# Small operations moved between engines, and the edges of two scan layers, in a four-layer state-space kernel

## The chip, the cores and the metric

The kernel runs on one core of a Trainium2 chip. A core has five engines that run beside each other, each through its own instructions in order: TensorE (PE, with its weight loads as PEld), VectorE (DVE), ScalarE (ACT), GpSimd (POOL) and SyncE (SP), which here issues all DMAs. The metric is the device time of one execution in microseconds, as the median of several runs.

## The reference

The input is 8 images of 48 x 48 pixels with 96 channels, in float32. Four layers follow each other, each as `x = x + layer(group_norm(x))`.

Layers 0 and 3 (`ss2d` in the kernel) are 2D selective scans. A projection gives 2 x 192 channels, u and z. u goes through a 3 x 3 depthwise convolution and a SiLU. The image is then read as a sequence in four directions (rows, columns, and both backward), and in each of them a recurrence with 16 states a channel is run:

```
dA = exp(dl[..., None] * A)
h = h * dA + (dl * u)[..., None] * Bv[:, :, None, :]
y = einsum('bkdn,bkn->bkd', h, Cv)
...
y = sum of the four directions, back in image order, plus D * u
y = (y - mean(y)) * rsqrt(var(y) + 1e-5) * norm_w + norm_b
out = (y * silu(z)) @ out_proj.T
```

`dl` (softplus of a small projection), `Bv` and `Cv` are projections of u. Layer 2 (`lines`) does the same recurrence along each row or column separately, restarts it at every line, gates each direction by silu(z), projects it and adds it to x. Layer 1 (`spectral`) upsamples by Fourier, applies a small network and downsamples.

## The kernel before

The four layers run one after the other. An image (a "job") has 4 directions of 5 blocks each: `BLKS` cuts it into four blocks of 10 rows or columns (480 pixels) and one of 8 (384). A scan layer is thus a list of 8 x 4 x 5 blocks, made in `scans`, direction after direction.

A block has 192 channels x 16 states = 3072 sequences, kept as 24 units of 128 partitions. It goes through 8 slots of 3 units (two slots are a turn `t`, 4 turns are a block, 160 slots an image). For each turn the code issues, in this order by engine:

- VectorE: three recurrences of two units (`scan`, L263, `tensor_tensor_scan` in place in the tile dbu), and between them the products dl * u * B (`make_dbu`, L235).
- ScalarE: the decays exp(dl * A) into a PSUM tile (`make_da`, L255), two units at a time, with two buffers, so that the decays of a scan can be made while the scan before it runs; and a copy of B into PSUM (`copy_b`, L216).
- GpSimd: a part of the products dl * u * B (L235, the table `ON_POOL`), and h * C in place (`make_hc`, L276).
- TensorE: the sum over the 16 states, as matmuls with a 0/1 matrix into the PSUM tile y (`reduce`, L296 and L298). It comes one turn after the scans.
- SyncE: loads of B and C for the next block (`load_bc`, L204) and of dl and dl * u (`load_dd`, L192), broadcast over partitions.

Everything else is fitted in by `aside`, which is called once a slot. It issues the loads of that slot, takes one step of the generator `beside` (which `side(job)` makes), then runs the steps of `stage1` that prepare the block after next (`plan`), then the steps that `done` has put aside. Nothing is scheduled by the machine: the order in which the code issues instructions is the order of each engine, and the framework only adds the waits that the data and the buffers need. PSUM tiles of the name "side" have one buffer.

In `ss2d`, `side(job)` does for the image before: `post`, the norm over channels, gate and output projection; and for the image after: load, `front` (group norm) and `conv` (the 3 x 3 convolution as nine 128-column matmuls a half block, L481, with SiLUs at L490 and L492). `post` has two loops over the 5 blocks. The first takes the mean (L504), subtracts it (L507), squares (L510), sums by matmul (L515) and copies the variance (L518), five steps a block; then square root and reciprocal of the whole image (L520, L522). The second, from slot 30 on, again takes five steps a block:

```
step 1: z <- zd, xi <- x by DMA (L528, L530); PE repeats 1/sigma over the partitions (L534)
step 2: DVE y *= norm_w * 1/sigma, two instructions (L538)
step 3: POOL y *= z (L541); PE norm_b part of the projection (L544)
step 4: PE projection of y (L547)
step 5: DVE xi += result (L550)
then:   store of xi by DMA (L552), before step 1 of the next block
```

The tile zin has one buffer, xi has two. The last image has no image after it, so its `post` runs after the scans, alone. The first image's `front` and `conv` run before the scans, alone.

In `lines`, `done` multiplies y by silu(z) on VectorE (L785), `project` multiplies by the output weights a slot later (L794), and `add` adds the result to x on VectorE, one more slot later (L800 for direction 0, with the bias; L802 for the others). Directions 2 and 3 go by columns, so x is then read and written with a stride.

Of the kernel before, what the change touches and what calls it, by code (L numbers as in the profile page):

```python
# [17 lines left out]
DH = 96  # L18
# [57 lines left out]
def vss_stack_kernel(ctx: ExitStack, tc: tile.TileContext, i: dict, out: bass.AP):  # L76
# [89 lines left out]
    def scans(dirs, restart, a, pools, ps, stage1, opening, done, side, tail):  # L166
# [9 lines left out]
                  for job in range(nb) for k in range(NK)  # L176
# [171 lines left out]
        for t, (b, q) in enumerate(turns):  # L348
            at, nblk = 2 * t, t // (NG // 2)
            if q == 0:  # L350
                if nblk + 2 < len(blocks):
                    plan(blocks[nblk + 2], at)
                if b.k == 0 and b.first:
                    beside = side(b.job)
# [24 lines left out]
            if q == NG // 2 - 1 and b.k == NK - 1 and b.last:  # L379
                for _ in beside:  # L380
                    while tail:
                        tail.pop(0)()
# [47 lines left out]
    def ss2d(l, xin, xout, b0=0):  # L430
# [65 lines left out]
        def post(b):  # L496
            y = yss[b]
            var = small.tile([CH, L // CH], F32, tag="var", name="var")
            for r0, nr in BLKS:
# [20 lines left out]
            nc.scalar.activation(var, var, AF.Sqrt, bias=eps5[:CH])  # L520
            yield
            nc.vector.reciprocal(var, var)  # L522
            yield
            for r0, nr in BLKS:
# [7 lines left out]
                for c in range(n // CH):  # L532
                    at = r0 * W // CH + c
                    nc.tensor.matmul(pr[:DH, c * CH:(c + 1) * CH], lhsT=var[:, at:at + 1].to_broadcast([CH, DH]),  # L534
                                     rhs=wc["ident"], start=True, stop=True)
                yield
# [4 lines left out]
                nc.gpsimd.tensor_mul(y[:, :, s], y[:, :, s], z[:, :, :n])  # L541
# [8 lines left out]
                nc.vector.tensor_add(xi[:, :n], xi[:, :n], po[:C, :n])  # L550
                yield
                nc.sync.dma_start(xout[b][:, s], xi[:, :n])  # L552

        def side(job):
            used = 0
            more = job + 1 < nb
            if more:
# [9 lines left out]
            if more:  # L567
# [6 lines left out]
                yield from conv(job + 1)  # L574
# [74 lines left out]
    def lines(xin, xout):  # L649
# [131 lines left out]
        def done(b, half, y):  # L781
# [7 lines left out]

            def project():  # L790
                got["o"] = ps("s1", 2)
                t = gated.pop(b)
                for h in range(2):
                    nc.tensor.matmul(got["o"][:C, :n], lhsT=wo[:, b.k, h, :], rhs=t[:, h, :n], start=(h == 0), stop=(h == 1))  # L794
# [27 lines left out]
        scans(dirs, True, a, pools, ps, stage1, opening, done, side, tail)  # L822
# [289 lines left out]
```

## Time and profile before

| what | value |
|---|---|
| median of 3 runs | 19549.3 us (19545.86 to 19551.5) |
| the profiled execution | 19542.61 us, span 19540.6 us |
| first scan layer: first scan, last scan's end | 148.7 us, 5902.6 us |
| `lines`: first scan of the layer | 7397.6 us |
| last scan layer: first scan | 13675.7 us |
| VectorE L263, the recurrences | 5760 instructions, 11858.2 us busy |
| GpSimd L276, h * C | 3840 instructions, 11439.8 us busy |
| ScalarE L255, the decays | 11520 instructions, 7414.7 us busy |
| TensorE L296 and L298 | 30720 records, 4983.6 and 4942.9 us busy |

The page gives the busy time of each engine, the groups of instructions by source line with the idle time before them and what ended it, and the chain of work that ended last. The windows view sums busy time in stretches of time, the waits view lists who waited for whom, and the timeline lists instructions in order; its columns are start, duration, engine, line, operation, output and inputs, and the idle time before it with its releaser in brackets. A float32 matmul shows as two records. Most of the time lies in three long, even scan stages (two of `ss2d`, one of `lines`), so what one image costs there counts eight times.

### The profile page before, as it was taken

The numbers are of one execution on the slowest core, as the hardware profiler recorded it, in microseconds if no ns is written. First come the engines' busy times: TensorE is split into PE (matmuls) and PEld (weight loads), VectorE is DVE, ScalarE is ACT, GpSimd is POOL, SyncE is SP. The second block draws the span as 40 slices with busy tenths as digits, with TensorE's granted clock in tenths as the row PEclk, the third lists the DMA queues.
The fourth block names the chain that finished last, engine by engine and source line by source line (L and its number), as shares of the span: only waits on it lengthen the run. The fifth ranks groups of instructions, "written<-read, shape, count | busy, mean of one in ns | idle before, by whom it ended". The sixth has DMA issues, their size and how long they took to land. (4 is left out here: it accounts for less than half of the span.)

```text
span 19540.6 us, 172984 instructions
## 1 busy us (share of the span) xinstructions
PE 15237.1 (78%) x53500; PEld 4370.8 (22%) x53500; DVE 16831.8 (86%) x11281; ACT 14144.5 (72%) x22222; POOL 16028.7 (82%) x9825
## 2 busy tenths in 40 slices
PE   6777777777767887888888988887677777777776
PEld 1211211211214552222222222222121121121121
DVE  6999999999992228999999999996999999999997
ACT  5877777877772227788788777885778778778775
POOL 6999999999991007888888888886999999999997
PEclk6777776776767777888878888887677677667765
DMA  3444444444443324434434444443444444444443
GB/s 130 160 162 158 162 160 163 158 163 158 156 170 48 50 45 145 145 141 150 150 139 147 147 146 145 144 149 112 158 163 160 159 164 157 160 162 161 156 165 123
DMA packets 768486, 2829.44 MB, mean 145 GB/s; under 512 B 235724, under 2 KB 298668, under 8 KB 640926
## 3 DMA queue, kind: packets, MB, share of 16 engines
q1 hardware_dynamic: 767558, 2818.38, 43.1%
q8 instruction: 422, 6.91, 0.1%
q14 instruction: 506, 4.15, 0.1%
HBM read 2371.42 MB, written 446.69 MB: 144 GB/s over the span
## 5 line engine op out<-in xcount | busy, mean ns | idle before, releaser
L263 DVE TENSOR_TENSOR_SCAN dbu<-ps_da,dbu 128x962 f32<-128x962 f32 (+3 forms) x5760 | 11858.2, 2071 | 897.9 <-ACT ps_da L255 895.7
L276 POOL TENSOR_TENSOR dbu<-dbu,bc 128x1440 f32<-128x1440 f32 (+1 forms) x3840 | 11439.8, 2985 | 1040.6 <-DVE dbu L263 814.0
L255 ACT ACTIVATE ps_da<-dd,w_l_a 128x481 f32<-128x481 f32 (+3 forms) x11520 | 7414.7, 648 | 2729.7 <-DVE dbu L263 2523.7
L296 PE MATMUL ps_y<-dbu,w_red 128*32 128x480 f32 (+1 forms) x23040 | 4983.6, 752 | 3051.0 <-POOL dbu L276 3047.3
L298 PE MATMUL ps_y<-dbu,w_red 128*32 128x480 f32 (+1 forms) x7680 | 4942.9, 752 | 0.0
L235 DVE TENSOR_TENSOR dbu<-dd,ps_b 128x1440 f32<-128x1440 f32 (+5 forms) x3840 | 4645.3, 1210 | 320.1 <-ACT ps_b L216 275.7
L235 POOL TENSOR_TENSOR dbu<-dd,bc 128x480 f32<-128x480 f32 (+3 forms) x1920 | 3026.2, 1576 | 61.9 <-DMA bc<-bcd 36.6
L296 PEld LDWEIGHTS ps_y<-dbu,w_red 128*32 128x32 f32 x23040 | 742.7, 125 | 7009.7 <-POOL dbu L276 5283.6
L216 ACT COPY ps_b<-bc 128x480 f32<-128x480 f32 (+1 forms) x3360 | 1798.4, 535 | 300.7 <-DVE dbu L235 271.3
L722 PE MATMUL ps_s<-xpad,w_l_cw 128*128 128x480 f32 (+1 forms) x2560 | 1747.2, 834 | 2.3 <-ACT xpad L124 1.6
L481 PE MATMUL ps_side<-xpad,w_l_cw 128*128 128x480 f32 (+1 forms) x2880 | 1617.4, 690 | 4.6 <-ACT xpad L124 4.5
L255 ACT ACT_TABLE_LOAD x970 | 1244.5, 1283 | 17.1
L113 POOL MEMSET w_l_cw<- 128x1760 f32 (+1 forms) x3 | 5.8, 1942 | 1326.7 <-DVE x L932 1321.3
L422 POOL TENSOR_TENSOR dds<-dds,u 96x480 f32<-96x480 f32 (+1 forms) x640 | 793.6, 1240 | 259.9 <-ACT dds L611 259.9
L593 PE MATMUL ps_s<-u,w_l_xp 96*38 96x480 f32 (+1 forms) x1280 | 957.2, 888 | 4.1 <-ACT dds L587 3.0
L583 PE MATMUL ps_s<-bcl,dtw 6*96 6x480 f32 (+1 forms) x1280 | 878.4, 775 | 86.3 <-ACT dds L587 82.2
L270 POOL COPY carry<-dbu 128x3 f32<-128x3 f32 x2048 | 386.4, 189 | 582.6 <-DVE dbu L263 570.2
L292 PE MATMUL ps_y<-ysum,w_ident 96*96 96x480 f32 (+1 forms) x960 | 740.7, 861 | 113.7 <-ACT ysum L634 112.8
L481 PEld LDWEIGHTS ps_side<-xpad,w_l_cw 128*128 128x128 f32 x2880 | 571.0, 222 | 1115.0 <-issue 916.4
L722 PEld LDWEIGHTS ps_s<-xpad,w_l_cw 128*128 128x128 f32 x2560 | 525.8, 210 | 1087.1 <-issue 938.1
L298 PEld LDWEIGHTS ps_y<-dbu,w_red 128*32 128x32 f32 x7680 | 683.1, 125 | 0.0
L763 PE MATMUL ps_s<-xpad,w_l_inz 96*96 96x480 f32 (+1 forms) x640 | 505.7, 924 | 86.9 <-ACT dds L757 69.2
(146 smaller groups left out, 12586.2 us busy)
## 6 DMA issues: line engine op xcount, KB each, us to landing
dd<-dd SPq DMA_DIRECT2D x512, 1443.0 KB
bc<-bcd SPq DMA_DIRECT2D x1536, 480.0 KB
dd<-dd SPq DMA_DIRECT2D x256, 1440.0 KB
dd<-dds SPq DMA_DIRECT2D x512, 360.8 KB
dd<-dd SPq DMA_DIRECT2D x128, 1155.0 KB
bc<-bcd SPq DMA_DIRECT2D x384, 384.0 KB
dd<-dds SPq DMA_DIRECT2D x256, 360.0 KB
dd<-dd SPq DMA_DIRECT2D x64, 1152.0 KB
```

What stands on the lines that cost most here:

```text
L216: nc.scalar.copy(bps[t][:, :b.n], bcs[t][:, 0, :b.n])
L235: engine.tensor_mul(o, du, by.unsqueeze(1).to_broadcast([P, hi - lo, b.n]))
L255: nc.scalar.activation(da[:, at:at + b.m], b.got[half][:, u % 3, 0, :], AF.Exp, scale=a[:, b.k, ci:ci + 1])
L263: nc.vector.tensor_tensor_scan(db, da, db, 0.0, ALU.mult, ALU.add)
L276: nc.gpsimd.tensor_mul(h, h, bcs.pop(2 * t + sub)[:, 1, :n].unsqueeze(1).to_broadcast([P, 3, n]))
L296: nc.tensor.matmul(y[32 * g:32 * g + 32, :n], lhsT=wc["red"][:, :32], rhs=hc[:, g, b.at], start=False, stop=(slot == 3))
L298: nc.tensor.matmul(y[DH:, :n], lhsT=wc["red"][:, 32:], rhs=hc[:, 2, b.at], start=(slot == 0), stop=(slot == 3))
L422: nc.gpsimd.tensor_mul(rows(du, n), rows(dt, n), u)
L481: nc.tensor.matmul(pu[:, :n], lhsT=flat[:, at:at + P], rhs=xpad[:, r0 + dy:r0 + dy + nr, dx:dx + W], start=(tap == 0), stop=(tap == 8))
L583: nc.tensor.matmul(got["p"][:DH, :n], lhsT=dtw[2 * NS:, b.k, half, :], rhs=b.bcl[2 * NS:, :n], start=True, stop=True)
L593: nc.tensor.matmul(got["p"][:NBC, :n], lhsT=w[f"{l}_xp"][:, b.k, half, :], rhs=u[:, half], start=(half == 0), stop=(half == 1))
L722: nc.tensor.matmul(got["u", half][:, :n], lhsT=flat[:, at:at + P], rhs=shifted(off), start=(tap == 0), stop=(tap == 3))
```

## The change

In `ss2d`:

- The norm weight is multiplied into the rows of the output weights once a layer, on ScalarE. In `post`'s second loop y * z on GpSimd now stands in step 1, and 1/sigma is applied after the projection: step 2 copies 1/sigma from PSUM (ACT), step 3 projects y * z (PE), step 4 multiplies the two (DVE), step 5 sums xi, the norm_b part and the result in PSUM by four matmuls, two of them with the identity (PE); a copy on ACT takes it out, followed at once by the store of xi and by step 1 of the next block.
- `post` takes a list of blocks. The last image's blocks 4 to 1 go through it one by one beside the last direction, two steps a slot; block 0 alone runs after the scans. For that the order of directions is 0, 1, 3, 2, so that the last one goes by rows, backward, and finishes block 4 first.
- `conv` of the first image does three blocks before the scans; the last two, two fifths, stand beside the first two blocks of scans, two steps a slot.

In `lines`, x joins the projection in PSUM as an identity matmul, and ScalarE copies the sum into x (with the bias for direction 0), in place of VectorE's addition.

```diff
--- before.py
+++ after.py
@@ -163,7 +163,7 @@
         yield
 
 
-    def scans(dirs, restart, a, pools, ps, stage1, opening, done, side, tail):
+    def scans(dirs, order, restart, a, pools, ps, stage1, opening, done, side, tail):
 
 
 
@@ -173,7 +173,7 @@
 
 
         blocks = [Block(job, k, blk, n == 0, n == len(BLKS) - 1, dirs[k][1])
-                  for job in range(nb) for k in range(NK)
+                  for job in range(nb) for k in order
                   for n, blk in enumerate(range(len(BLKS))[::-1 if dirs[k][1] else 1])]
         for b in blocks:
             b.columns(restart)
@@ -350,7 +350,7 @@
             if q == 0:
                 if nblk + 2 < len(blocks):
                     plan(blocks[nblk + 2], at)
-                if b.k == 0 and b.first:
+                if b.k == order[0] and b.first:
                     beside = side(b.job)
             scan(t, 0)
             if t > 0:
@@ -376,7 +376,7 @@
             copy_b(at + 4)
             finish(at + 1)
             aside(at + 1)
-            if q == NG // 2 - 1 and b.k == NK - 1 and b.last:
+            if q == NG // 2 - 1 and b.k == order[-1] and b.last:
                 for _ in beside:
                     while tail:
                         tail.pop(0)()
@@ -450,9 +450,12 @@
         taps = flat[:DH, :9 * 2 * DH].rearrange("p (t e) -> p t e", t=9)
         nc.vector.tensor_mul(taps, taps, w[f"{l}_in"][:, :2 * DH].unsqueeze(1).to_broadcast([DH, 9, 2 * DH]))
 
+
         wnb = wt.tile([DH, 2, C], F32, tag="wnb", name="wnb")
         for half in range(2):
             nc.scalar.activation(wnb[:, half, :], w[f"{l}_out"][:, half, :], AF.Identity, scale=w[f"{l}_nb"][:, half:half + 1])
+            wo = w[f"{l}_out"][:, half, :]
+            nc.scalar.activation(wo, wo, AF.Identity, scale=w[f"{l}_nw"][:, half:half + 1])
         xpad = wt.tile([P, H + 2, W + 2], F32, tag="xpad", name="xpad")
         nc.gpsimd.memset(xpad, 0.0)
         us, yss, zs = {}, {}, {}
@@ -467,10 +470,11 @@
         def load_x(b):
             nc.sync.dma_start(xpad[:C, 1:1 + H, 1:1 + W], seq(xin[b], False))
 
-        def conv(b):
-            us[b] = big.tile([DH, 2, L], F32, tag="big", name="u")
-            zs[b] = zdr.tile([DH, 2, L], F32, tag="z", name="zd")
-            for r0, nr in BLKS:
+        def conv(b, blks):
+            if blks[0] == BLKS[0]:
+                us[b] = big.tile([DH, 2, L], F32, tag="big", name="u")
+                zs[b] = zdr.tile([DH, 2, L], F32, tag="z", name="zd")
+            for r0, nr in blks:
                 n = nr * SEG
                 for half in range(2):
                     pu = side_psum()
@@ -493,10 +497,12 @@
                     yield
                     nc.sync.dma_start(zs[b][:, half, s], z[:, :n])
 
-        def post(b):
+        def post(b, blks=BLKS):
+
             y = yss[b]
             var = small.tile([CH, L // CH], F32, tag="var", name="var")
-            for r0, nr in BLKS:
+            v0, v1 = min(r0 for r0, nr in blks) * W // CH, max(r0 + nr for r0, nr in blks) * W // CH
+            for r0, nr in blks:
                 n = nr * SEG
                 s = slice(r0 * W, r0 * W + n)
                 pm = side_psum()
@@ -517,11 +523,11 @@
                 yield
                 nc.vector.tensor_copy(var[:, r0 * W // CH:(r0 * W + n) // CH], pv[:CH, :n // CH])
                 yield
-            nc.scalar.activation(var, var, AF.Sqrt, bias=eps5[:CH])
+            nc.scalar.activation(var[:, v0:v1], var[:, v0:v1], AF.Sqrt, bias=eps5[:CH])
             yield
-            nc.vector.reciprocal(var, var)
+            nc.vector.reciprocal(var[:, v0:v1], var[:, v0:v1])
             yield
-            for r0, nr in BLKS:
+            for r0, nr in blks:
                 n = nr * SEG
                 s = slice(r0 * W, r0 * W + n)
                 z = lnp.tile([DH, 2, BMAX], F32, tag="zin", name="zin", bufs=1)
@@ -533,27 +539,35 @@
                     at = r0 * W // CH + c
                     nc.tensor.matmul(pr[:DH, c * CH:(c + 1) * CH], lhsT=var[:, at:at + 1].to_broadcast([CH, DH]),
                                      rhs=wc["ident"], start=True, stop=True)
-                yield
-                for half in range(2):
-                    nc.vector.scalar_tensor_tensor(y[:, half, s], y[:, half, s], w[f"{l}_nw"][:, half:half + 1], pr[:DH, :n],
-                                                   ALU.mult, ALU.mult)
-                yield
                 nc.gpsimd.tensor_mul(y[:, :, s], y[:, :, s], z[:, :, :n])
+                yield
+                t = lnp.tile([DH, 2, BMAX], F32, tag="sq", name="normed", bufs=1)[:, 0, :n]
+                nc.scalar.copy(t, pr[:DH, :n])
+                yield
                 po = side_psum()
                 for half in range(2):
-                    nc.tensor.matmul(po[:C, :n], lhsT=wnb[:, half, :], rhs=z[:, half, :n], start=(half == 0), stop=False)
-                yield
+                    nc.tensor.matmul(po[:C, :n], lhsT=w[f"{l}_out"][:, half, :], rhs=y[:, half, s],
+                                     start=(half == 0), stop=(half == 1))
+                yield
+                nc.vector.tensor_mul(t, t, po[:C, :n])
+                yield
+                po = side_psum()
+                nc.tensor.matmul(po[:C, :n], lhsT=wc["ident"], rhs=xi[:, :n], start=True, stop=False)
                 for half in range(2):
-                    nc.tensor.matmul(po[:C, :n], lhsT=w[f"{l}_out"][:, half, :], rhs=y[:, half, s],
-                                     start=False, stop=(half == 1))
-                yield
-                nc.vector.tensor_add(xi[:, :n], xi[:, :n], po[:C, :n])
-                yield
+                    nc.tensor.matmul(po[:C, :n], lhsT=wnb[:, half, :], rhs=z[:, half, :n], start=False, stop=False)
+                nc.tensor.matmul(po[:C, :n], lhsT=wc["ident"], rhs=t, start=False, stop=True)
+                yield
+                nc.scalar.copy(xi[:, :n], po[:C, :n])
                 nc.sync.dma_start(xout[b][:, s], xi[:, :n])
 
         def side(job):
             used = 0
             more = job + 1 < nb
+            if job == 0:
+                for n, _ in enumerate(conv(0, BLKS[3:])):
+                    if n % 2:
+                        used += 1
+                        yield
             if more:
                 load_x(job + 1)
             if job > 0:
@@ -571,7 +585,17 @@
                 while used < 10 * NG:
                     used += 1
                     yield
-                yield from conv(job + 1)
+                yield from conv(job + 1, BLKS)
+            else:
+
+                for n, blk in enumerate(BLKS[:0:-1]):
+                    while used < (NK * len(BLKS) - len(BLKS) + n + 1) * NG + 2:
+                        used += 1
+                        yield
+                    for m, _ in enumerate(post(job, [blk])):
+                        if m % 2:
+                            used += 1
+                            yield
 
         def stage1(b):
             n = b.n
@@ -638,10 +662,10 @@
         load_x(0)
         for _ in front(0):
             pass
-        for _ in conv(0):
+        for _ in conv(0, BLKS[:3]):
             pass
-        scans(dirs, False, a, pools, ps, stage1, opening, done, side, [])
-        for _ in post(nb - 1):
+        scans(dirs, (0, 1, 3, 2), False, a, pools, ps, stage1, opening, done, side, [])
+        for _ in post(nb - 1, BLKS[:1]):
             pass
         stack.close()
 
@@ -787,19 +811,22 @@
                 return []
             got = {}
 
+            xv = seq(xs[b.job], dirs[b.k][0])[:, b.r0:b.r0 + b.nr, :]
+
             def project():
+
                 got["o"] = ps("s1", 2)
                 t = gated.pop(b)
+                nc.tensor.matmul(got["o"][:C, :n], lhsT=wc["ident"], rhs=xv, start=True, stop=False)
                 for h in range(2):
-                    nc.tensor.matmul(got["o"][:C, :n], lhsT=wo[:, b.k, h, :], rhs=t[:, h, :n], start=(h == 0), stop=(h == 1))
+                    nc.tensor.matmul(got["o"][:C, :n], lhsT=wo[:, b.k, h, :], rhs=t[:, h, :n], start=False, stop=(h == 1))
 
             def add():
-                xv = seq(xs[b.job], dirs[b.k][0])[:, b.r0:b.r0 + b.nr, :]
                 v = rows(got["o"][:C], n)
                 if b.k == 0:
-                    nc.vector.scalar_tensor_tensor(xv, v, w["l2_outb"], xv, ALU.add, ALU.add)
+                    nc.scalar.activation(xv, v, AF.Identity, bias=w["l2_outb"])
                 else:
-                    nc.vector.tensor_add(xv, xv, v)
+                    nc.scalar.copy(xv, v)
                 if b.k == NK - 1 and b.last:
                     nc.sync.dma_start(xout[b.job], xs[b.job])
 
@@ -819,7 +846,7 @@
         load_x(0)
         for _ in front(0):
             pass
-        scans(dirs, True, a, pools, ps, stage1, opening, done, side, tail)
+        scans(dirs, range(NK), True, a, pools, ps, stage1, opening, done, side, tail)
         stack.close()
```

More of the change, by code (lines that the diff above doesn't have):

```diff
@@ L535, in post @@
                                      rhs=wc["ident"], start=True, stop=True)
+                nc.gpsimd.tensor_mul(y[:, :, s], y[:, :, s], z[:, :, :n])
                 yield
-                for half in range(2):
-                    nc.vector.scalar_tensor_tensor(y[:, half, s], y[:, half, s], w[f"{l}_nw"][:, half:half + 1], pr[:DH, :n],
-                                                   ALU.mult, ALU.mult)
+                t = lnp.tile([DH, 2, BMAX], F32, tag="sq", name="normed", bufs=1)[:, 0, :n]
+                nc.scalar.copy(t, pr[:DH, :n])
                 yield
-                nc.gpsimd.tensor_mul(y[:, :, s], y[:, :, s], z[:, :, :n])
                 po = side_psum()
                 for half in range(2):
-                    nc.tensor.matmul(po[:C, :n], lhsT=wnb[:, half, :], rhs=z[:, half, :n], start=(half == 0), stop=False)
+                    nc.tensor.matmul(po[:C, :n], lhsT=w[f"{l}_out"][:, half, :], rhs=y[:, half, s],
+                                     start=(half == 0), stop=(half == 1))
                 yield
+                nc.vector.tensor_mul(t, t, po[:C, :n])
+                yield
+                po = side_psum()
+                nc.tensor.matmul(po[:C, :n], lhsT=wc["ident"], rhs=xi[:, :n], start=True, stop=False)
                 for half in range(2):
-                    nc.tensor.matmul(po[:C, :n], lhsT=w[f"{l}_out"][:, half, :], rhs=y[:, half, s],
-                                     start=False, stop=(half == 1))
+                    nc.tensor.matmul(po[:C, :n], lhsT=wnb[:, half, :], rhs=z[:, half, :n], start=False, stop=False)
+                nc.tensor.matmul(po[:C, :n], lhsT=wc["ident"], rhs=t, start=False, stop=True)
                 yield
-                nc.vector.tensor_add(xi[:, :n], xi[:, :n], po[:C, :n])
-                yield
+                nc.scalar.copy(xi[:, :n], po[:C, :n])
                 nc.sync.dma_start(xout[b][:, s], xi[:, :n])
```

## The prediction

> **What bounds the kernel now.** I read the page first, then busy time by windows, the waits, and timelines of one image and of the end. The page:
>
> ```profile
> PE 15237.1 (78%) x53500; PEld 4370.8 (22%) x53500; DVE 16831.8 (86%) x11281; ACT 14144.5 (72%) x22222; POOL 16028.7 (82%) x9825
> ```
>
> VectorE leads, GpSimd follows closely. Three windows of the first layer, by columns: length, then busy time of PE, PEld, DVE, ACT, POOL, then the granted clock. First, two blocks with nothing beside the scans; then slots 30 to 55 of image 1 (the second loop of `post`); then two blocks with the convolution beside.
>
> ```profile
> 227.70:296.80 69.10, 46.02 (x148) 7.32 (x152) 68.03 (x41) 53.99 (x91) 65.47 (x47) 0.52 0.44 149
> 993.10:1116.90 123.80, 96.30 (x342) 25.56 (x342) 114.75 (x82) 86.81 (x145) 113.87 (x74) 0.68 0.52 174
> 1205.60:1278.70 73.10, 51.72 (x203) 13.12 (x204) 68.04 (x46) 58.87 (x104) 66.96 (x49) 0.79 0.52 184
> ```
>
> Bare scans are VectorE's (68.03 of 69.10). In `post`'s second loop GpSimd is as full as VectorE: 113.87 against 114.75, so it has 9.9 us to spare in 123.8. Who makes VectorE wait:
>
> ```profile
> DVE dbu L263 <- ACT ps_da L255: 895.7, 840, 4.4
> ACT bcl L598 <- PE ps_s L593: 457.9, 219, 5.8
> ```
>
> ScalarE is late with the decays, partly because it stood waiting for TensorE, which in its turn waits in order for GpSimd's products (L276). A late GpSimd thus reaches VectorE by way of PE and ACT. How `post` hides its load today, in image 1:
>
> ```profile
> 1037.19 0.63 DVE L550 TENSOR_TENSOR xi<-xi,ps_side 96x480 f32<-96x480 f32 x1
> ...
> 1038.25 0.60 SPq L528 DMA_DIRECT2D zin<-zd  x1
> ...
> 1040.85 2.06 POOL L235 TENSOR_TENSOR dbu<-dd,bc 128x960 f32<-128x960 f32 x1
> ...
> 1051.86 2.22 POOL L541 TENSOR_TENSOR ysum<-ysum,zin 96x960 f32<-96x960 f32 x1
> ```
>
> and at the end of the kernel, where nothing hides it:
>
> ```profile
> 19494.34 0.62 SPq L528 DMA_DIRECT2D zin<-zd  x1
> ...
> 19498.66 2.21 POOL L541 TENSOR_TENSOR ysum<-ysum,zin 96x960 f32<-96x960 f32 x1 [9.05 <-DMA zin<-zd]
> ```
>
> From issue to use 4.3 us pass; in image 1 GpSimd has 13.6 us, since its multiply stands two slots behind the load.
>
> [...] while L541 waits 9.05 us, nothing of GpSimd passes it. [...]
>
> **Part by part.** A slot is one call of `aside`, about 4.5 us; an image has 160.
>
> (a) *`post` beside the scans, 14 images (7 in each scan layer).* Removed per block: two L538 of 0.70 us; the add L550 (0.65) gives way to a multiply of the same form. VectorE saves 1.4 us a block, 5 x 1.4 x 0.96 (the last block is 384 wide) = 6.7 us an image. ACT gets two copies of 0.55 us a block; at slot 31 the saved STT pair lets the next scan start only 0.25 us earlier, since its decays end at 1002.35. PE gets two identity matmuls a block: two records of 0.40 us each at the fast clock, 0.80 at the slow one, 1.6 to 3.2 us.
>
> The cost lies in the order. The GpSimd multiply moves two slots forward, into the slot that issues its load. That load (L528's successor) stands on SP behind the store of the block before, which now waits for an ACT copy, which waits for four matmuls emitted one slot earlier (3.3 to 6.5 us). For blocks 2 to 5 of an image GpSimd therefore arrives before the data: slot 40: GpSimd is there at 1042.9 (end of the 2.06 us piece above); ACT is free for the copy at 1042.9; plus 0.55 copy, 0.45 to the issue, 4.2 to landing = 1048.1, a stall of 5.2. Slot 35: arrival 1021.1; PE reaches the four matmuls at 1020.9, ends at 1024.3 at the fast clock; + 0.55 + 0.45 + 4.2 = 1029.5: 8.4. With GpSimd and PE already late, PE's chain (reduction 1.7, matmuls 3.3, copy and issue 1.0, landing 4.2 = 10.2 from the product) against GpSimd's own 6 us to the multiply leaves 4. I bound a stall by 4 and 8.5 and take 6: 4 x 6 = 24 us an image. Block 1 has no store ahead of its load and no stall. Behind the waiting multiply stand the products L276, behind these PE's reductions, behind those `raw`, s0 and the new output matmuls, on which ACT and VectorE wait.
> Cover: GpSimd's 9.9 us. The loop becomes GpSimd's: 113.9 + 24 = 138 against 123.8, +14; some of its 9.9 us idle stays (it also waits for scans): +15. VectorE's saving is in the shade of this. From 4 x 4 to 4 x 8.5 the range is +6 to +24. 14 x 15 = **+210** (84 to 336).
>
> (b) *`lines`, 160 blocks.* VectorE loses the adds: L802 120 and L800 40 times, 129 us (all but the last), and the idle time before them, in the answer on L802:
>
> ```profile
>   PE ps_s L794: 82.8, 73
> ```
>
> and 32.9 for L800: at most 245 us. But ACT takes over both, copy (0.55 by rows, 0.98 by columns as in L634) and wait. I followed each block in the timeline: from the end of ACT's instruction before the next decays, or the end of L794 plus one identity matmul (half of L794's time, mean 1.3 us), plus copy, plus decays, to the second scan after the add: 0.44 us earlier on average: -70. The identity matmul also pushes the next block's convolution (L722) back; there are hardly gaps in PE up to the Silu L729, and in 71 blocks ACT then is up to 1.76 us late: +83. Sum **+13**; from -70 (PE catches up) to +83 (nothing gained).
>
> (c) *The last image's `post`, both layers.* Today it stands alone from 19438.6 to 19537.7, 99 us. Alone stays one block: 3.0 + 1.2 + 1.0 + 3.0 (L504, L507, L510, L515) + 0.9 (deviation) + 1.9 (L534) + 0.6 + 2.3 + 0.7 + 4 (four matmuls) + 0.6 = 19: -80. Beside the scans come four blocks, each: 2.1 us VectorE (1.15 + 0.17 + 0.16 + 0.65), some 1.7 because the subtraction follows its matmul within one slot, 3.2 because ACT waits for the variance and loads two tables (2 x 1.28), 3 for the output matmul behind a later GpSimd: 10. 4 x 10 = 40. Net -40 a layer, **-80** (-110 to -40). L0's tail is as exposed: spectral's first loads follow it on SP at 6007.
>
> (d) *Two fifths of the first convolution, both layers.* Four half blocks go from the head: 2 x 8.3 + 2 x 6.7 = -30 (L481's 7.51 or 6.07 us plus matmul, Silu and turn). Beside scans a half block costs today (73.1 - 69.1)/2 = 2, here 4 x 2 = 8 plus PE overflow: at the clock 0.79, two bare blocks are 46.0 x 0.52/0.79 = 30, four half blocks 2 x (51.7 - 30) = 43; 73 of 77 us fits barely, at a lower clock not: 7. Net -15 a layer, **-30** (-50 to 0).
>
> (e) *Order of directions, weight scaling:* same blocks and sizes, two more ACT instructions of 0.3 us a layer at the head: 0.
>
> Sum: 210 + 13 - 80 - 30 = +113. The span 19540.6 becomes 19653.6; the profiled run took 19542.6, 6.7 below the median 19549.3. Predicted median: 19549 + 113 = **19662**.
>
> **The rivals.** *GpSimd's wait is covered, faster:* if the load lands before GpSimd arrives, because GpSimd itself runs late enough in the scans, VectorE's saving counts, say 4 of 6.7 us: 14 x -4 = -56, lines -70, tails -110, heads -40: 19273. It decides where the sum of stalls stays under the 9.9 us of slack. For it: L541 never waits in the scans today. Against it: the store and the load now hang on the slot's own ACT copy. *Break-even:* stalls at 4 us: 14 x 6 = +84, lines 0, tails and heads -100: 19533. *Worse:* stalls of 8.5 and PE late in `lines`: 336 + 83 - 60: 19908.
>
> **From cases to numbers.** Forecast 0.55, its own range 19590 to 19790; covered 0.18; break-even 0.15; worse 0.12. Faster or slower means by more than 0.2%, 39 us, about what a measurement of this kernel can tell. Of the forecast's chance a little falls under 39 us. Range 19420 to 19850: it leaves out most of the covered case and the far end of the worse one. Faster 0.19, same 0.16, slower 0.65.
>
> **What would show it.** In the waits after, the GpSimd multiply of `post` waits for zin some 56 times for 4 to 8 us each, 250 to 450 us in all; GpSimd's L276 and VectorE's new multiply in `post` wait for their predecessors longer. Slots 30 to 55 take about 139 us. After the last scan 20 us stand instead of 100. In `lines` the add's wait is found on ACT. I am wrong if the multiply does not wait, or if PE and ACT don't hand its delay on to VectorE.

## The result and the profile after

The changed kernel takes 19788.3 us (median; 19775.5 to 19789.9), beside 19547.6 for the kernel before on the same chip: a ratio of 1.0122, interval 1.0104 to 1.0139, so +241 us where +113 was forecast. The profiled execution took 19789.89 us, with a span of 19788.1.

The page of the changed kernel, first part:

```profile
PE 15452.1 (78%) x54140; PEld 4484.3 (23%) x54140; DVE 16640.6 (84%) x10969; ACT 14331.6 (72%) x22586; POOL 16014.8 (81%) x9825
```

VectorE has 191 us less to do than before, and GpSimd as much as before. TensorE has 215 us more and ScalarE 187 us more, but both stay under 80% of the span. So the page alone does not tell where the 241 us come from.

To find that out I cut both traces at the starts of the scans (L263; 80 turns are an image). Lengths in us:

| stretch | before | after | difference |
|---|---|---|---|
| head, layer 0 / between layer 2 and 3 | 148.7 / 157.2 | 118.9 / 131.1 | -29.8 / -26.0 |
| image 0, layer 0 / layer 3 | 705.3 / 704.9 | 714.8 / 713.9 | +9.5 / +9.0 |
| images 1 to 6, layer 0 / layer 3 | 4353.1 / 4354.6 | 4488.5 / 4478.5 | +135.4 / +123.8 |
| image 7, layer 0 / layer 3 | 695.5 / 697.4 | 749.2 / 743.3 | +53.7 / +45.9 |
| tail of layer 0 with `spectral` / tail of layer 3 | 1495.0 / 108.0 | 1443.5 / 31.4 | -51.5 / -76.6 |
| `lines` | 6120.9 | 6175.0 | +54.1 |

In images 1 to 6 nearly all of the loss, 21.6 us an image, lies in slots 32 to 55, where `post`'s second loop runs. In image 7 these slots take 23.6 and 21.2 us more, and the blocks of the last direction, with the new posts of one block beside them, 28.9 and 24.2. By the terms of the prediction: (a) 135.4 + 123.8 + 23.6 + 21.2 = +304; (b) +54; (c) 28.9 + 24.2 - 51.5 - 76.6 = -75; (d) -29.8 - 26.0 + 9.5 + 9.0 = -37. The four give +246; the spans of the two profiled executions differ by 247.5, the medians by 241.

Slots 30 to 55 of image 1 in the changed kernel, by the same columns as before: start and end, length, busy PE, PEld, DVE, ACT, POOL, granted clock, DMA share, GB/s.

```profile
973.80:1118.50 144.70, 105.22 (x360) 28.92 (x362) 109.59 (x73) 89.33 (x154) 113.62 (x74) 0.70 0.45 148
```

144.7 us stand where 123.8 stood. GpSimd's 113.6 are unchanged, so its idle time went from 9.9 to 31.1 us. What it waits for in that window, first in the kernel before (in total, times, longest):

```profile
POOL carry L270 <- DVE dbu L263: 5.7, 5, 1.9
POOL dbu L276 <- DVE dbu L263: 2.8, 4, 1.4
```

and after:

```profile
POOL ysum L542 <- DMA zin<-zd: 22.0, 5, 5.7
POOL carry L270 <- DVE dbu L263: 4.0, 2, 2.4
POOL dbu L276 <- DVE dbu L263: 3.7, 2, 3.0
```

The new wait for z is 22.0 us, the window grew by 20.9, and the waits for VectorE's scans are nearly what they were: 8.5 us before, 7.7 after. The same five waits stand in each of the 14 images; in image 1 they are 1.1, 5.7, 5.7, 5.1 and 4.4 us, and over the images their sum is 19.1 to 23.8, in all 308.3 us. The wait reaches VectorE at two places. Its longest waits in the same window, before:

```profile
DVE dbu L263 <- ACT ps_da L255: 6.8, 4, 4.4
DVE xi L550 <- PE ps_side L547: 2.8, 1, 2.8
```

and after:

```profile
DVE normed L552 <- PE ps_side L549: 18.7, 3, 8.0
DVE dbu L263 <- ACT ps_da L255: 17.0, 9, 6.6
```

L552 is the multiply that took the place of the old add L550. VectorE waits 26.1 us longer at these two, which is the 20.9 us of the window and the 5.2 us of work that VectorE no longer has. How one of GpSimd's waits for z comes about, in the timeline of the changed kernel (slot 40; start, length, engine, line, and in brackets the idle time before it with its releaser):

```profile
1025.84 1.36 ACT L255 ACTIVATE ps_da<-dd,w_l_a 128x481 f32<-128x481 f32 x2
1027.51 2.06 POOL L235 TENSOR_TENSOR dbu<-dd,bc 128x960 f32<-128x960 f32 x1
1027.65 1.37 ACT L255 ACTIVATE ps_da<-dd,w_l_a 128x481 f32<-128x481 f32 x2 [0.45 <-DVE dbu L263]
1029.20 0.56 ACT L216 COPY ps_b<-bc 128x480 f32<-128x480 f32 x1 [0.18 <-DVE dbu L235]
1029.69 0.55 ACT L560 COPY xi<-ps_side 96x480 f32<-96x480 f32 x1
...
1030.27 0.31 SPq L561 DMA_DIRECT2D x<-xi  x1
...
1030.67 0.60 SPq L534 DMA_DIRECT2D zin<-zd  x1
...
1035.23 2.23 POOL L542 TENSOR_TENSOR ysum<-ysum,zin 96x960 f32<-96x960 f32 x1 [5.66 <-DMA zin<-zd]
```

GpSimd is ready at 1029.57. The load is issued at 1030.67, directly behind the store L561, which stood on SP until the copy L560 was done. The copy in its turn stood on ScalarE behind decays and the copy of B. From issue to use 4.56 us pass. Everything in brackets at L542 is time in which GpSimd's queue stands: in this trace nothing of GpSimd runs between 1029.57 and 1035.23.

Lines of the waits view of the whole span:

```profile
DVE dbu L263 <- ACT ps_da L255: 1209.9, 1138, 8.0
POOL ysum L542 <- DMA zin<-zd: 315.5, 72, 7.2
DVE normed L552 <- PE ps_side L549: 292.9, 52, 8.3
ACT x L829 <- PE ps_s L822: 137.1, 93, 14.0
```

The scans wait 314 us longer for decays than before (895.7 there), and L552 waits 292.9 us for the projection of the late product, where the old add L550 waited 110.2. Not all of the 314 belongs to z: the experiments below show 136 of it in `lines`. The last line is the add of `lines`, which waits on ScalarE now.

The end of the changed kernel, with the last scan first:

```profile
19754.62 2.13 DVE L263 TENSOR_TENSOR_SCAN dbu<-ps_da,dbu 128x962 f32<-128x962 f32 x1
...
19768.50 2.21 POOL L542 TENSOR_TENSOR ysum<-ysum,zin 96x960 f32<-96x960 f32 x1 [7.33 <-ACT sq L516]
...
19784.46 0.55 ACT L560 COPY xi<-ps_side 96x480 f32<-96x480 f32 x1 [10.30 <-PE ps_side L558]
```

One block of `post` is left after the scans, and the kernel ends 31.4 us after the last scan instead of 108.0.

### The profile page after: what moved, and what is told of

Read it like the earlier page. It is cut to its first block, busy times and chain, and to the rows that moved or that the text cites. A ratio compares the mean times of both kernels' runs of the same rounds, so it can differ in the third digit from the quotient of the medians.

```text
span 19788.1 us, 174246 instructions
## 1 busy us (share of the span) xinstructions
PE 15452.1 (78%) x54140; PEld 4484.3 (23%) x54140; DVE 16640.6 (84%) x10969; ACT 14331.6 (72%) x22586; POOL 16014.8 (81%) x9825
## 4 chain that ended last, share of the span: by engine, by line
DVE 27%; PE 20%; POOL 19%; ACT 14%; issue 12%; DMA 7%; SPq 0%; POOLq 0%; DVEq 0%; ACTq 0%
DVE dbu L263 17%; POOL dbu L276 14%; DVE dbu L235 9%; ACT ps_da L255 4%; PE ps_s L746 4%; PE ps_y L296 3%; ACT L255 3%; DMA dd<-dd 2%; POOL dds L422 2%; POOL dbu L235 2%; PE ps_h L979 2%; DMA dd<-dds 2%; PE ps_s L617 2%; PE ps_y L992 1%; PE ps_s L822 1%
## 5 line engine op out<-in xcount | busy, mean ns | idle before, releaser
L263 DVE TENSOR_TENSOR_SCAN dbu<-ps_da,dbu 128x962 f32<-128x962 f32 (+3 forms) x5760 | 11849.7, 2069 | 1211.4 <-ACT ps_da L255 1209.9
L296 PE MATMUL ps_y<-dbu,w_red 128*32 128x480 f32 (+1 forms) x23040 | 4870.2, 738 | 3165.3 <-POOL dbu L276 3160.7
L298 PE MATMUL ps_y<-dbu,w_red 128*32 128x480 f32 (+1 forms) x7680 | 4829.0, 738 | 0.0
```

The costliest lines, as they stand in the source:

```text
L263: nc.vector.tensor_tensor_scan(db, da, db, 0.0, ALU.mult, ALU.add)
L296: nc.tensor.matmul(y[32 * g:32 * g + 32, :n], lhsT=wc["red"][:, :32], rhs=hc[:, g, b.at], start=False, stop=(slot == 3))
L298: nc.tensor.matmul(y[DH:, :n], lhsT=wc["red"][:, 32:], rhs=hc[:, 2, b.at], start=(slot == 0), stop=(slot == 3))
```

## The experiments

Theory 1: GpSimd's wait for z is the whole of term (a), and goes into the span in full. The rival: the loss in these slots has another cause, such as the added matmuls and copies. Times are medians beside the kernel before on the same chip: 19550.9 in the first four runs, 19552.4 in the next four, 19545.9 in the last two.

**z a block earlier.** The kernel after, with z of the next block loaded while this one is worked on (and xi loaded two slots later, into one buffer):

```
+            def load_z(blk):
...
+                t = lnp.tile([DH, 2, BMAX], F32, tag="zin", name="zin", bufs=2)
+                nc.sync.dma_start(t[:, :, :m], zs[b][:, :, at:at + m])
...
-                z = lnp.tile([DH, 2, BMAX], F32, tag="zin", name="zin", bufs=1)
-                nc.sync.dma_start(z[:, :, :n], zs[b][:, :, s])
...
+                z = zin
+                zin = load_z(blks[blks.index((r0, nr)) + 1]) if (r0, nr) != blks[-1] else None
```

Expected: 

> The changed kernel, but z of the next block is loaded a whole block (five slots) earlier into a second buffer, and xi has one buffer and is loaded two slots later; order and arithmetic of PE, DVE and ACT stay. Theory 1 (in post's second loop GpSimd stands waiting for z, and that delay goes through PE and ACT to VectorE): the stalls of 4 to 7 us at the GpSimd multiply go away beside the scans, slots 30 to 55 of an image fall from 144.6 to about 126 us, and 14 images x 19 us give about 19520 (19480 to 19600). Rival (the four output matmuls in one step and the ACT copies that wait for them make the loss, and GpSimd's wait only fills time that it would have lost anyway): slots 30 to 55 stay above 138 us and the time above 19700.

Measured: 19495.1, a ratio to before of 0.9972 (0.9961 to 0.9982), 293 us under the kernel after. The same slots of image 1, and what is left of the wait in the whole span:

```profile
971.10:1093.90 122.80, 98.74 (x362) 27.20 (x362) 109.45 (x72) 90.09 (x153) 112.89 (x74) 0.77 0.52 174
```

```profile
POOL ysum L547 <- DMA zin<-zd: 26.3, 16, 6.6
```

The wait has nearly gone, and the window is back at 122.8 us, with all the added matmuls and copies still in it. The rival falls. Over the 14 images these windows take 1747.7 us, against 2023.5 in the kernel after and 1723.9 before. So 276 of the 300 us come back. VectorE has 5.3 us less to do in each window than before (109.45 against 114.75 in image 1), and the windows are still 1.7 us longer on average: VectorE's work does not set their length.

**The multiply a slot later.** The kernel after, one step moved:

```
-                nc.gpsimd.tensor_mul(y[:, :, s], y[:, :, s], z[:, :, :n])
                 yield
+                nc.gpsimd.tensor_mul(y[:, :, s], y[:, :, s], z[:, :, :n])
                 t = lnp.tile([DH, 2, BMAX], F32, tag="sq", name="normed", bufs=1)[:, 0, :n]
```

Expected: 

> The changed kernel, with the GpSimd multiply y * z put one slot later (step 2 instead of step 1), nothing else. Theory 1: some 4.5 us more between load and use take most of a stall of about 5 us away, slots 30 to 55 take about 130 us and the whole about 19580 (19530 to 19650). Rival (PE's matmuls and ACT's copies): no gain, 19750 or more, since the output matmul of step 3 now has its product one slot later.

Measured: 19531.5 (0.9991; 0.9984 to 0.9997), at the low end of the expected range. The waits of this kernel:

```profile
DVE normed L552 <- PE ps_side L549: 156.3, 45, 6.4
...
POOL ysum L543 <- DMA zin<-zd: 60.2, 53, 2.7
```

One slot of distance takes four fifths of the wait for z (315.5 to 60.2). In the windows of slots 30 to 55 of the 14 images, 140.7 us of the wait at L552 remain, beside 87.9 with z a block earlier and 37.4 for the old add. The 53 us between the first two are what I would put down to the order here, as the projection follows a product that was made only a slot before; no run separates it.

**The load ahead of the store.** The kernel after, with the load in the multiply's own slot still, but issued before the store of the block before and into a second buffer (xi again loaded two slots later):

```
-                z = lnp.tile([DH, 2, BMAX], F32, tag="zin", name="zin", bufs=1)
+                z = lnp.tile([DH, 2, BMAX], F32, tag="zin", name="zin", bufs=2)
                 nc.sync.dma_start(z[:, :, :n], zs[b][:, :, s])
...
+                if held:
+                    nc.sync.dma_start(xout[b][:, held[0]], held[1][:, :held[2]])
...
-                nc.sync.dma_start(xout[b][:, s], xi[:, :n])
+                held = (s, xi, n)
```

Expected: 

> The kernel after, with one thing changed in the second loop of post: each block's z load stays in the slot of its multiply, but it goes to SP ahead of the store of the block before and into a second buffer, so that it no longer stands behind a store that waits for an ACT copy, nor for the matmuls that read the old z; the load of xi moves two slots later to make room. Theory 1 (the stall is mostly the queue: store behind copy behind matmuls; the load itself, 4.3 us, is largely passed while GpSimd works off its own pieces): GpSimd's wait for zin falls from 7.2 us a block to 2 or less, and most of the gain of the earlier load (19495) comes: 19550, 19510 to 19620. Rival (the multiply in the load's own slot is enough, whatever stands ahead of the load): the wait stays at 5 us or more and the time at 19700 or above.

Measured: 19547.8 (0.9999; 0.9991 to 1.0007). In its waits:

```profile
POOL ysum L543 <- DMA zin<-zd: 107.9, 44, 6.6
```

107.9 of 315.5 us stay. So the place behind the store and the one buffer, which this run changes together, make up two thirds of the wait, if the load stays in the multiply's own slot; and the distance of one slot alone took four fifths. The two overlap, and the wait cannot be split between them. The distance in the program and the queue are both parts of the cause, and either one mended takes 240 us or more of the time after back.

**`lines` alone.** The kernel before with the change in `lines` only (its part of the diff).

Expected: 

> The kernel before with the change in lines alone: identity matmul for x, ACT copies instead of VectorE's addition. From the traces of before and after the eight images of lines take 6120.9 and 6175.0 us, so if the parts add up: 19548 + 54 = 19602 (19580 to 19625). If lines is slower only because it comes behind a changed first layer [...], it stays at 19550.

Measured: 19605.7 (1.0025; 1.0015 to 1.0035), +55. Term (b) stands for itself, and does not come from GpSimd's waits in other layers.

**`lines`, TensorE's part only.** The kernel before, with a matmul whose sum the next one overwrites:

```
             def project():
...
+                nc.tensor.matmul(got["o"][:C, :n], lhsT=wc["ident"], rhs=xv, start=True, stop=True)
                 for h in range(2):
```

Expected: 

> The kernel before, with an identity matmul put ahead of the two output matmuls of lines; its sum is overwritten and brings nothing, and VectorE adds as before. So only TensorE's part of the change in lines is there. Theory 1 (the prediction's split: the PE part costs +83 us, the move of the add to ACT gains 30 or more against it; the measured sum is +54): 19634, 19605 to 19665. Rival (the matmul is nearly free, as PE is idle for a quarter of the time, and the loss is ACT's, which takes over 160 copies and their waits): 19575 or below.

Measured: 19736.1 (1.0093; 1.0079 to 1.0106), +184. Both expectations miss: the matmul is far from free, and costs twice what the prediction gave it. In this kernel the rows of the identity matmul and of VectorE's adds (busy and mean; then the idle time before them):

```profile
L795 PE MATMUL ps_s<-x,w_ident 96*96 96x480 f32 (+1 forms) x320 | 261.0, 908 | 25.7 <-ACT zb L771 24.0
...
L804 DVE TENSOR_TENSOR x<-x,ps_s 96x480 f32<-96x480 f32 (+1 forms) x120 | 102.8, 857 | 223.2 <-PE ps_s L797 222.8
...
L802 DVE SCALAR_TENSOR_TENSOR x<-ps_s,w_l_outb,x 96x480 f32<-96x480 f32 (+1 forms) x40 | 27.7, 693 | 59.0 <-PE ps_s L797 58.6
```

261 us of TensorE stand between the gate and the add, and VectorE's wait for the sum grows from 82.8 + 32.9 to 222.8 + 58.6 us, by 166 of the 184. TensorE's share of 78% says nothing of this place: here its work lies in the chain.

The add on ScalarE takes 184 - 55 = 129 us of that back. That is the difference of two runs; ScalarE's part cannot be built without the matmul. Why it is no more than that, in the waits of the kernel before

```profile
DVE gated L785 <- PE ps_y L298: 34.8, 54, 6.4
ACT ub L729 <- PE ps_s L722: 58.0, 56, 4.6
```

and of the run with `lines` alone:

```profile
DVE dbu L263 <- ACT ps_da L255: 1031.3, 1034, 4.4
DVE gated L785 <- PE ps_y L298: 161.7, 97, 6.4
ACT ub L729 <- PE ps_s L722: 71.2, 68, 4.6
```

VectorE is freed of 130 us of adds and 116 us of waiting for them. The scans wait 136 us longer for decays (895.7 before), and the gate 127 us longer for the sum over states. The 246 us freed came back as 263 us of other waits. The two do not close to the 55 us, because the adds overlap their neighbours: in the layer, VectorE's busy time falls by 103 us (5634.1 to 5530.8), its idle time grows by 147, and the layer by 44 (6120.9 to 6164.9 in these traces). The gate's longer wait is not made by the matmul alone: with TensorE's part only it is 40.5 us. It appears in the kernels in which VectorE no longer adds.

**The edges alone.** The kernel before, with the posts by blocks, the order 0, 1, 3, 2 and the split convolution; the arithmetic of `post` and `lines` as before.

Expected: 

> The edges of the change alone: post by blocks beside the last direction with the order 0, 1, 3, 2, and two fifths of the first convolution beside scans; post's arithmetic and lines as before. If the parts add up, the two edges bring what they brought in the change: -75 for the tails, -37 for the heads, 19548 - 112 = 19436 (19410 to 19470). If the new arithmetic of post is what makes the short tail possible, the gain is smaller: 19480 or more, because the old second loop has two more VectorE instructions a block beside the last direction.

Measured: 19437.1 (0.9939; 0.9927 to 0.9952), -114. Terms (c) and (d), -75 and -37 by the table, are confirmed in their sum, and this half of the change alone beats the kernel before. The short tail does not need the new arithmetic: 31.3 us stand after the last scan here too.

**The arithmetic of `post` alone**, in the kernel before.

Expected: 

> The kernel before, with the new second loop of post alone (scaled weights, GpSimd multiply first, two copies on ACT, identity matmuls); order of directions, split of the convolution and lines as before. Theory 1 (14 posts beside scans lose 21.8 us each by GpSimd's wait, independent of the other parts; the two last posts, alone at the end of a layer, have a somewhat longer chain of dependent steps, 10 us each): 19550 + 305 + 20 = 19875, 19840 to 19910. Rival (a part of the 21.8 us belongs to the other order and the split): 19800 or below.

Measured: 19911.0 (1.0181; 1.0167 to 1.0195), +359, 1 us above the expected range. In its trace images 1 to 7 lose 301 us in the two layers (130.6 + 127.1 + 21.3 + 22.5), as theory 1 says. The tails were mis-sized: layer 3's is 140.1 us instead of 108.0, +32, and the stretch with layer 0's tail grew by 46, where I had given 10 each.

**All but the loss.** The kernel after, with z a block ahead from the head of `post` on, and with the old adds in `lines`:

```
             y = yss[b]
...
+            zin = load_z(blks[0])
             var = small.tile([CH, L // CH], F32, tag="var", name="var")
```

Expected: 

> The kernel after, with z loaded a block ahead (the first block's at the head of post, so also in the last image's posts of one block each) and with the old adds in lines. Theory 1: the earlier load gave 19495; the old lines take 54 off; the blocks of the last direction, which waited for z in posts of one block, lose some 4 us less each, 2 layers x 4 blocks x 4 = 32: 19410, 19380 to 19440. Against the edges alone (19437) it shows what the new arithmetic of post brings when its wait is gone: nothing in the 14 posts, where GpSimd is the bound. Rival (VectorE's 6.7 us an image do count once the wait is gone): 19340 or below.

Measured: 19432.1 (0.9938; 0.9925 to 0.995). It cannot be told from the edges alone (19437.1). The new arithmetic of `post` brings nothing measurable even with its wait gone; the rival falls. These two kernels are the fastest of the study, 0.6% under the kernel before.

**Work added to GpSimd.** The prediction took GpSimd's 9.9 us of idle time as cover. To test that by itself: the kernel with z a block earlier, and in the posts beside scans a copy of a half block onto itself, once or three times a block. It changes no value.

```
+                if len(blks) == len(BLKS):
+                    for _ in range(1):
+                        nc.gpsimd.tensor_copy(y[:, 0, s], y[:, 0, s])
                 nc.gpsimd.tensor_mul(y[:, :, s], y[:, :, s], z[:, :, :n])
```

Expected of one: 

> The kernel with the earlier z load (19495), and in the 14 posts beside scans one GpSimd copy of a half block onto itself ahead of each multiply of the second loop: work that changes no value and that no one waits for but GpSimd's own queue. The trace of before has no such copy; from the copy of 3 columns (0.19 us) and the multiply of 960 (2.2 us) I bound it by 0.4 and 1.1 us and take 0.7, so some 3.4 us an image, well under the 8 us that GpSimd is idle in slots 30 to 55. Theory 1 (that idle time is handover from VectorE's scans and covers nothing: what GpSimd gets there is added to the span one for one): 14 x 3.4 = +47, so 19542, 19522 to 19572, or 70 times the traced duration of a copy. Rival (the idle time is a cover, as the prediction took it): 19495, at most 19510.

Expected of three: 

> As the run with one copy a block, with three copies: some 10 us an image. Theory 1 (one for one): 3 x 47 = +141, so 19636, 19580 to 19720, and three times the rise of the run with one copy. Rival (8 us of idle time cover): 14 x 2 = +28, so 19523.

Measured: 19531.5 (0.9991; 0.9983 to 0.9999) and 19588.1 (1.0022; 1.0015 to 1.003). The copies in the two traces:

```profile
L549 POOL COPY ysum<-ysum 96x480 f32<-96x480 f32 (+1 forms) x70 | 39.6, 566 | 0.0
```

```profile
L549 POOL COPY ysum<-ysum 96x480 f32<-96x480 f32 (+1 forms) x210 | 119.0, 566 | 8.6
```

Against the kernel before of their own chip the three kernels stand at -55.9, -14.4 and +42.2 us, each known to some 15 to 20 us. So 39.6 us of copies cost 41 us, and 119.0 cost 98. A copy takes 0.566 us on average and not the 0.7 I had set, which is why both times lie under the expected middle; the last one still lies in its range, and the rival's values (19510 and 19523) are missed. Slots 30 to 55 of image 1 with three copies a block:

```profile
973.50:1105.30 131.80, 105.22 (x362) 28.24 (x362) 109.46 (x73) 89.04 (x153) 121.82 (x89) 0.69 0.50 163
```

GpSimd is idle for 131.80 - 121.82 = 10.0 us of it, as it was for 9.9 us before. Image 1 alone could mislead, so here are the sums over the 14 windows of slots 30 to 55, cut at the starts of the scans, in us:

| kernel | length | GpSimd busy | its wait for z | its other idle time | VectorE's wait for decays | VectorE's wait for the projection |
|---|---|---|---|---|---|---|
| before | 1723.9 | 1593.0 | 0 | 130.9 | 88.7 | 37.4 |
| after | 2023.5 | 1588.5 | 308.3 | 126.7 | 233.5 | 261.5 |
| z a block earlier | 1747.7 | 1587.1 | 18.5 | 142.1 | 106.7 | 87.9 |
| and one copy | 1778.9 | 1624.0 | 9.3 | 145.6 | 101.2 | 134.8 |
| and three copies | 1845.3 | 1705.1 | 0.6 | 139.6 | 132.5 | 180.7 |

The other idle time, 9.1 to 10.4 us an image, hardly moves, whether GpSimd stands 308 us for z or has 118 us more to do. What three copies save of their cost, 20 us in these windows, is about what was left of the wait for z, which a later GpSimd no longer meets. In the kernel before, 109.6 of the 130.9 us are waits for VectorE's scans: the idle time is mostly the handover from them, and it came again in each of these kernels (99.0 to 109.6 us).

The last column shows where a late GpSimd is paid for. From z a block earlier to three copies, VectorE's wait for the projection grows by 92.8 us, nearly the 97.6 us of the windows, and its wait for decays by 25.8. The multiply that waits there stands in VectorE's queue ahead of scans. Whether the idle time would cover something if that multiply stood a slot later was not tried.

## Why the prediction was right and wrong

The direction was right, and the time lies in the range. The size was not: +241 against +113. Two terms account for it, (a) by 94 us and (b) by 41.

**(a), the failing step.** "Cover: GpSimd's 9.9 us. The loop becomes GpSimd's: 113.9 + 24 = 138 against 123.8, +14". The wait before this line was right. It was forecast as four of 6 us, 24 us an image; there are five, four of about 5.2 us and one of 1.1, 22.0 in image 1. Slot 40 was worked out as 5.2 and has 5.66; slot 35 as 8.4 and has 5.68. Some 250 to 450 us were named for the waits in all; 315.5 were found. Then I took 9 of 24 us off for idle time, because GpSimd was busy for only 113.9 of 123.8 us. I had written that some of the idle time stays because GpSimd also waits for scans, and gave that 1 us an image; 9 us stayed. Nothing was to be taken off: the loss is the wait, 22 us an image, 304 in all instead of 210, and slots 30 to 55 take 144.7 us where about 139 were named. The miss would have been larger, 9 x 14 = 126 us, had the waits not been 2 us an image shorter than forecast.

The idle time was in the waits of the kernel before, where it could have been read: 8.5 of the 9.9 us are waits for VectorE's scans. That VectorE and GpSimd wait for each other in turn, so that a late GpSimd makes the next scan late, and this makes GpSimd wait again, fits the waits; the copies show the result, not that mechanism in each slot. The path by which GpSimd's delay comes to VectorE was forecast: by the decays and by the new output matmuls. Of the 369 us that VectorE waits longer in the 14 windows, 145 stand at the decays and 224 at the multiply L552, which waits for these matmuls. One detail differs: in slot 40 the copy ahead of the store was held up by decays on ScalarE's queue, as the working of that slot had it, and not by the four matmuls that the general account names.

VectorE's saving in (a) "is in the shade": right. With the wait gone the windows are 1.7 us longer than before on average, for 5.3 us less work.

**(b), mis-sized, with the loss in another place.** The sum was +13 and is +54. In the forecast, -70 is what the second scan after the add gains, with the identity matmul already in the path to ScalarE's copy; +83 is ScalarE's delay at the Silu L729, because the next convolution stands behind that matmul. By the waits of the run with `lines` alone, the first was larger: 246 us freed, 136 us more waiting for decays, so some 110 gained and not 70. The second was much smaller: the wait at L729 grows by 13 us, not 83. What the forecast does not have is the gate, L785, which waits 127 us longer for the sum over states. Why that sum is late for it is not shown. So the forecast's bounds of (b) held, but not by its reasons. The run with TensorE's part alone prices the matmul where VectorE still waits for its result, 184 us; this and the 129 us taken back are not the two terms of the forecast.

**(c), right in its sum, in part by luck**: -80 forecast, -75 found. The tails gave 128 us instead of 160, and the blocks beside scans cost 53 instead of 80, so two misses cancel. Layer 3's tail gave 76.6 of the 80, though one block alone takes 31.4 us after the last scan and not 20; its blocks beside scans cost 24.2 instead of 40. Layer 0's tail shows only 51.5, but that stretch holds `spectral` too, and its length varies by itself: the run with only TensorE's part of `lines` changes nothing in it and has +24.2, and the edges alone have -75.9 with the same edges. So the split of (c) by layers is uncertain by some 25 us.

**(d), right**: heads -29.8 and -26.0, forecast -30 each; image 0 +9.5 and +9.0, forecast 15. Its scaling of TensorE's time by the granted clock was an estimate. One pair of stretches in the trace of before agrees with it: the same two bare blocks of image 7 keep TensorE busy for 43.37 us at 0.55 in layer 0 and for 38.37 us at 0.63 in layer 3, and the products are 23.9 and 24.2. **(e)**, 0: nothing in the runs speaks against it.

Of the rivals, the covered case needed a sum of stalls under 9.9 us; it was 22, and even below that the cover would not have been there, as the run with one copy a block shows (39.6 us in 14 images, 2.8 us each, no cover seen beyond the noise of some 25 us). The case of 8.5 us stalls had a size for (a) near the truth, 336, for the wrong reason: stalls too long, less a cover that was not there.

What stays open: how the 129 us that ScalarE's add takes back divide into shorter waits and work moved; whether the identity matmul would be cheaper in an earlier slot, ahead of the gate; and whether GpSimd's idle time would cover a part if VectorE's new multiply stood later. None of it was tried.

## What to carry to other kernels

Before idle time of an engine is taken off a new stall, read what the engine waits for in it: if it is the partner with which it alternates, the idle time can come again. Here it did, 9.1 to 10.4 us an image in the five kernels of the table, and the stall counted in full (22.0 us of wait, 20.9 us of a longer window in image 1). A multiply that is moved into the slot of its own load cost here what was queued ahead of that load plus the landing (in slot 40 GpSimd stood for 5.66 us, 4.56 of them between issue and use); load a block ahead, or keep the slots between, before the consumer is moved. An engine's low share says nothing of a chain: an extra matmul just ahead of a result that VectorE waited for cost 184 us for 261 us of its own time.

## What the runs showed of the hardware

GpSimd's copy of a half block onto itself (96 x 480 floats, in the last block 96 x 384) takes 566 ns on average over 210 copies in the run with three copies, beside 2141 ns on average over 80 for its multiply of whole blocks, twice as wide, by a second operand: about half as much per element. In the kernel after, VectorE's multiply L552, of 96 x 480 by a second operand, takes 0.65 us and GpSimd's L542, of 96 x 960, takes 2.22, so VectorE's time per element is six tenths of GpSimd's. The granted clock of slots 30 to 55 of image 1 was 0.70 in the kernel after and 0.77 with z a block earlier, where the same matmuls (360 and 362 records) stood in 122.8 us instead of 144.7, so more densely. Over the 14 images of the kernel after it was 0.66 to 0.72, and over the whole spans of the two runs 0.753 and 0.759. I have no explanation for that.
